# Reciprocal roots on VectorE, and a decoder's last FFN quantised in 16-bit steps

## The chip, the cores and the metric

The kernel runs on one core of a Trainium2 chip, as one launch. The metric is the device time of a launch in microseconds. The time before is 2435.77 us, the median of 3 runs (2435.06 to 2436.54). TensorE (PE) does matmuls and transposes, VectorE (DVE) and ScalarE (ACT) the work between them, GpSimd (POOL) a few steps, and SyncE's queue (SP) most weight loads.

## The reference

The program is a decoder of four layers on x of 8 sequences of 112 tokens and 256 features. Each layer is an attention, a cross attention on a context of 375 tokens, and an FFN, each added to x. Each begins with a layer norm without parameters:

```python
def _layernorm(x, axis=-1, eps=1e-05):
    m = jnp.mean(x, axis=axis, keepdims=True)
    v = jnp.var(x, axis=axis, keepdims=True)
    return (x - m) / jnp.sqrt(v + eps)
```

Some sublayers have norms of their own besides. The last FFN quantises its three weights and both its activations in blocks of 16 neighbours along the last axis:

```python
def fake_quant_nvfp4(x, global_scale):
    xb = x.reshape(sh[:-1] + (sh[-1] // BLOCK, BLOCK))
    amax = jnp.max(jnp.abs(xb), axis=-1, keepdims=True)
    sc = jnp.clip(amax / FP4_MAX * global_scale, 0.0, FP8_MAX)
    sc8 = sc.astype(jnp.float8_e4m3fn).astype(jnp.float32)
    dq = sc8 / global_scale
    safe_dq = jnp.where(dq == 0.0, 1.0, dq)
    a = jnp.clip(jnp.abs(xb) / safe_dq, 0.0, FP4_MAX)
    q = jnp.sign(xb) * _FP4_VALS[jnp.digitize(a, _FP4_MIDS)]
    return (q * dq).reshape(sh)
```

With gate and up of shape 1024 x 256 and down of 256 x 1024, it computes `x + linear(silu(gate(x)) * up(x), down)`, where each linear quantises both its inputs.

## The kernel before, in words

x stays in SBUF with the 112 tokens on the partitions and (sequence, feature) along the free axis. The twelve sublayers run one after the other.

**Order.** Tile's scheduler lays out each engine's instructions ahead of time. It goes by the program's order as priority, by its own estimates of when inputs are ready, and by when memory comes free. Inside a `manual_schedule` block the named engines keep the program's order; instructions from outside such a block can be put between. So statistics of the next norm (L431, L432) stand among the instructions of an attention that is still running.

**Norms.** `stats` (L424) takes mean and variance of each sequence by two DVE instructions, then calls `rsqrt` (L410) once for all the sequences that it was given. `normalise` (L442) subtracts and scales, one DVE instruction a sequence (L445). `rsqrt` adds eps (L414), takes the square root on ScalarE (L415), the reciprocal on DVE (L416), and a Newton step in four DVE instructions (L418 to L421). It runs 35 times: 32 times on 4 columns, twice on 8, once on 24. ScalarE's functions come from tables of which one set is active at a time; where the next function is in another set, an ACT_TABLE_LOAD is put ahead of it. Square root, Exp, Silu, Gelu and Sigmoid take turns, so 75 loads stand in the trace, 29 of them on L415.

**Quotients.** `quantise` (L1968) works on up to 2048 columns at once. Maxima of the blocks of 16 by one reduction (L1985); nine instructions on one column per block that round the scale to 8 bits and take its reciprocal (L1987 to L2001); the product of values and reciprocals, a block's factor broadcast over its 16 columns (L2004); a clamp (L2005); rounding to 4-bit values by adding and subtracting a number taken from the exponent (L2007 to L2010); the product with the scale, which writes bf16 (L2011). All of it is DVE's, and fp32 but for the last output.

**Last FFN** (`l3_ffn`, L2060). All eight sequences are normalised at once. Then x is quantised by halves of four sequences (1024 columns), transposed on PE and copied by ScalarE. Then come the four pairs of sequences: for each sequence and each half of the 1024 hidden columns, gate and up (four bf16 matmuls), Silu on ScalarE (L2103), and the product on DVE (L2104); `quantise` on the pair's 2048 columns; sixteen transposes (L2113), two copies (L2117), the down matmuls, and the sum into x (L2121). No order is written out by hand here. The output leaves by one DMA at the end.

**Weights of that FFN** are loaded by GpSimd's queue, quantised (`rounded`, L2023) and transposed (`turned`, L2040) while the third layer's last stages run. Their order along the free axis is set on the host (L250).

The cross attention ahead of the last FFN (`cross`, L1089) is one `manual_schedule` block; each sequence's result is added to x one sequence late, at L484.

Of the kernel before, what the change touches and what calls it, by code (L numbers as in the profile page):

```python
# [21 lines left out]
I32 = mybir.dt.int32  # L22
BF16 = mybir.dt.bfloat16
AF = mybir.ActivationFunctionType
ALU = mybir.AluOpType
# [4 lines left out]
P = 128  # L30
# [83 lines left out]
def _weights(inp):  # L114
# [134 lines left out]
    ]  # L249
    raw = [_fm(f("gate_w")), _fm(f("up_w")), _fm(f("down_w"))]  # L250
    v3 = [
# [101 lines left out]
class _Kernel:  # L353
# [56 lines left out]
    def rsqrt(self, var, rows, n):  # L410

        nc, small = self.nc, self.small
        va, sd, rs, t = (self.t(small, [P, 24], tag)[:rows, :n] for tag in ("va", "sd", "rs", "nt"))
        nc.vector.tensor_scalar(va, var, EPS, None, ALU.add)  # L414
        nc.scalar.activation(sd, va, AF.Sqrt)  # L415
        nc.vector.reciprocal(rs, sd)  # L416

        nc.vector.tensor_tensor(t, rs, rs, ALU.mult)  # L418
        nc.vector.tensor_tensor(t, t, va, ALU.mult)
        nc.vector.tensor_scalar(t, t, -0.5, 1.5, ALU.mult, ALU.add)  # L420
        nc.vector.tensor_tensor(rs, rs, t, ALU.mult)  # L421
        return rs
# [1544 lines left out]

    def quantise(self, pool, src, dst, rows, n, gs, amax=None):  # L1968


        nc = self.nc
        nb = n // 16

        def blocks(a):
            return a.rearrange("p (k e) -> p k e", e=16)

        def bc(a):
            return a[:, :, None].to_broadcast([rows, nb, 16])

        def sm(tag):  # L1980
            return self.t(pool, [P, nb], f"q{tag}{nb}")[:rows]

        if amax is None:
            amax = sm("m")
            nc.vector.tensor_reduce(amax, blocks(src), AX.X, ALU.max, apply_absolute_value=True)  # L1985
        sc, st, z = sm("s"), sm("t"), sm("z")
        nc.vector.tensor_scalar(sc, amax, 1.0 / 6.0, gs, ALU.mult, ALU.mult)  # L1987
        nc.vector.tensor_scalar(sc, sc, 448.0, None, ALU.min)


        big = 1.5 * 2.0**23
        nc.vector.tensor_scalar(
            st.bitcast(I32), sc.bitcast(I32), 0x7F800000, None, ALU.bitwise_and
        )
        nc.vector.tensor_scalar(st, st, 0.125 * big, 2.0**-9 * big, ALU.mult, ALU.max)
        nc.vector.tensor_tensor(sc, sc, st, ALU.add)
        nc.vector.tensor_tensor(sc, sc, st, ALU.subtract)
        nc.vector.scalar_tensor_tensor(z, sc, 0.0, sc, ALU.is_equal, ALU.add)
        nc.vector.reciprocal(z, z)

        nc.vector.tensor_scalar(z, z, gs, 1.0 + 2.0**-23, ALU.mult, ALU.mult)  # L2001
        a = self.t(pool, [P, n], f"qa{n}")[:rows]
        m = self.t(pool, [P, n], f"qm{n}")[:rows]
        nc.vector.tensor_tensor(blocks(a), blocks(src), bc(z), ALU.mult)  # L2004
        nc.vector.tensor_scalar(a, a, 6.0, -6.0, ALU.min, ALU.max)  # L2005

        nc.vector.tensor_scalar(m.bitcast(I32), a.bitcast(I32), 0x7F800000, None, ALU.bitwise_and)  # L2007
        nc.vector.tensor_scalar(m, m, 1.0, 0.5 * big, ALU.max, ALU.mult)
        nc.vector.tensor_tensor(a, a, m, ALU.add)
        nc.vector.tensor_tensor(a, a, m, ALU.subtract)  # L2010
        nc.vector.tensor_tensor(blocks(dst), blocks(a), bc(sc), ALU.mult)  # L2011

    def l3_weights(self, pool, ps):
# [9 lines left out]
        def rounded(i, nk, no):  # L2023
            amax = self.t(pool, [P, P], "amax")
            nc.vector.tensor_reduce(
                amax, raws[i].rearrange("p (k e) -> p k e", e=16), AX.X, ALU.max, apply_absolute_value=True
            )
            top, gs = (self.t(pool, [P, 1], n) for n in ("top", "gs"))
            nc.vector.tensor_reduce(top, amax, AX.X, ALU.max)
            nc.gpsimd.partition_all_reduce(gs, top, P, bass_isa.ReduceOp.max)  # L2030
            nc.vector.reciprocal(gs, gs)
            nc.vector.tensor_scalar(gs, gs, 448.0 * 6.0, None, ALU.mult)
            nc.vector.reciprocal(self.igs[:, i : i + 1], gs)
            wqs[i] = self.t(pool, [P, no, nk * P], "wq", BF16)
            flat = wqs[i].rearrange("p o k -> p (o k)")
            for h in range(2):
                cols = slice(h * 1024, (h + 1) * 1024)
                self.quantise(pool, raws[i][:, cols], flat[:, cols], P, 1024, gs, amax[:, h * 64 : (h + 1) * 64])

# [20 lines left out]
    def l3_ffn(self):  # L2060
# [3 lines left out]
        with ExitStack() as ctx:  # L2064
# [10 lines left out]
            for i, j in enumerate((0, 0, 1)):  # L2075
                nc.vector.tensor_tensor(sc[:, i : i + 1], self.igs[:, i : i + 1], inv[:, j : j + 1], ALU.mult)
            self.normalise(self.x, self.xn)
            xq = self.t(acts, [P, NB, D], "xq", BF16)
            xqT = self.t(acts, [P, 2, T], "xqT", BF16)
            for half in range(2):  # L2080
                bs = slice(half * HB, (half + 1) * HB)
                flat = [a[:S, bs, :].rearrange("p b d -> p (b d)") for a in (self.xn, xq)]
                self.quantise(pool, *flat, S, HB * D, s_in[:S])
                tp = self.t(ps, [P, 2, HT], "tr16", BF16)
                for kc in range(2):
                    for j in range(HB):
                        nc.tensor.transpose(
                            tp[:, kc, j * S : (j + 1) * S],
                            xq[:S, half * HB + j, kc * P : (kc + 1) * P],
                            self.ident16[:S, :S],  # L2090
                        )
                nc.scalar.copy(xqT[:, :, half * HT : (half + 1) * HT], tp)
            for b0 in range(0, NB, 2):
                hid = self.t(work, [P, 2, 1024], "hid")[:S]
                for j in range(2):
                    xb = self.tokens(b0 + j, xqT)
                    for i in range(2):
                        gu = self.t(ps, [P, 2, 512], "gu")
                        cols = slice(i * 512, (i + 1) * 512)
                        for n, m in enumerate((g, u)):  # L2100
# [3 lines left out]
                        nc.vector.scalar_tensor_tensor(  # L2104
                            hid[:, j, cols], gu[:S, 1, :], sc[:S, 1:2], sg, ALU.mult, ALU.mult
                        )
                hq = self.t(work, [P, 2, 1024], "hq", BF16)[:S]
                flat = [a.rearrange("p b d -> p (b d)") for a in (hid, hq)]
                self.quantise(pool, *flat, S, 2048, s_down[:S])
                for j in range(2):  # L2110
                    tp = self.t(ps, [P, 8, S], "tr16", BF16)
                    for c in range(8):
                        nc.tensor.transpose(  # L2113
                            tp[:, c, :], hq[:, j, c * P : (c + 1) * P], self.ident16[:S, :S]
                        )
                    hT = self.t(work, [P, 8, S], "hqT", BF16)
                    nc.scalar.copy(hT, tp)  # L2117
                    y = self.t(ps, [P, 512], "y")[:S, :D]
                    self.mm(y, [(hT[:, c, :], d[:, c, :]) for c in range(8)])
                    x = self.x[:S, b0 + j, :]  # L2120
                    nc.vector.scalar_tensor_tensor(x, y, sc[:S, 2:3], x, ALU.mult, ALU.add)  # L2121

# [35 lines left out]
```

## Time and profile before

| What | Value |
| --- | --- |
| Median of 3 runs | 2435.77 us (2435.06 to 2436.54) |
| Profiled execution | 2432.16 us |
| Its span | 2430.4 us |
| Granted clock of TensorE, mean | 0.954 |
| Busy share: PE, DVE, ACT, POOL | 88%, 59%, 34%, 9% |
| Square roots (L415): table loads, busy | 29, 37.2 us |
| Last sequence of the cross attention added to x | 2306.37 to 2306.79 us |
| Last sum into x | 2424.03 to 2424.51 us |
| DVE busy from 2308 to 2342 us | 32.65 of 34 us |

Times in a view are counted from the start of the span. A group's row gives line, engine, operation, output and inputs by name, shapes, count, then busy us and mean ns of one, then idle us of that engine just before. A row of the timeline gives start, us, engine and the instruction, and in brackets the idle time before it and who ended it. The chain of waits goes back from the last instruction to what released each one. A row of a stretch gives busy us and number of instructions of PE, PEld, DVE, ACT and POOL, the granted clock, and DMA.

### The profile page before, as it was taken

What the parts mean: (1) busy time and instruction counts of PE and PEld (TensorE: products, weight loads), DVE (VectorE), ACT (ScalarE), POOL (GpSimd) and SP (SyncE); (2) the same over time, 40 slices, a digit from 0 to 9 for tenths busy, and PEclk for the clock granted to TensorE, in tenths of its full rate; (3) what the DMA queues carried; (4) which work ended last, traced back from release to release, by engine and by line L of the source; (5) the groups of instructions that cost most, each with busy time, mean ns of one, the idle gap of its engine ahead of it and who ended that gap; (6) DMA issues with size and microseconds to landing.
All of it is one profiled execution on the core that took longest, in us unless ns stands there. A gap on an engine that the chain in (4) does not pass through costs nothing.

```text
span 2430.4 us, 43101 instructions
## 1 busy us (share of the span) xinstructions
PE 2138.1 (88%) x17032; PEld 1268.6 (52%) x17032; DVE 1434.3 (59%) x3810; ACT 826.8 (34%) x2220; POOL 215.8 (9%) x415
## 2 busy tenths in 40 slices
PE   6999999889899899899988859899999999899842
PEld 3444444455556566546555536466555556556622
DVE  4555556565446567553877547767740223667698
ACT  2333334453312356430111213467321111346521
POOL 0111111000011100000222331100000000100000
PEclk9999999999999999999999979999999999899966
DMA  4000000000100000100001011000111100000000
GB/s 185 2 2 2 2 20 35 29 18 18 52 1 15 18 1 2 36 26 18 35 18 35 18 28 52 17 2 19 53 35 62 41 1 1 1 1 2 2 1 15
DMA packets 10729, 55.93 MB, mean 23 GB/s; under 512 B 1833, under 2 KB 3625, under 8 KB 5792
## 3 DMA queue, kind: packets, MB, share of 16 engines
q1 hardware_dynamic: 8304, 44.57, 5.1%
q0 software_dynamic: 2080, 7.07, 0.9%
q8 instruction: 135, 2.21, 0.4%
q10 hardware_dynamic: 144, 1.54, 0.2%
q14 instruction: 66, 0.54, 0.1%
HBM read 52.23 MB, written 0.92 MB: 22 GB/s over the span
## 4 chain that ended last, share of the span: by engine, by line
PE 66%; DVE 22%; issue 5%; ACT 4%; DMA 2%; POOL 1%; DVEq 0%; ACTq 0%; POOLq 0%
PE mm L407 31%; PE tr L1178 6%; PE gu L407 6%; PE g L640 6%; PE sc L407 4%; PE av L1194 3%; PE tr L407 1%; DVE rot L1487 1%; PE av L777 1%; ACT sg L651 1%; PE av L407 1%; ACT th L662 1%; PE s L407 1%; DVE hT L666 1%; DMA cx<-in_ctx 1%
## 5 line engine op out<-in xcount | busy, mean ns | idle before, releaser
L640 PE MATMUL g<-w,hT 128*32 128x256 f32 x3552 | 237.4, 384 | 26.0 <-DVE hT L666 24.6
L1178 PEld LDWEIGHTS tr<-cst,xe 112*125 112x125 f32 x1152 | 151.5, 188 | 96.7 <-issue 37.0
L1165 DVE TENSOR_REDUCE xnm<-sc 112x1 f32<-112x375 f32 x384 | 184.3, 540 | 29.5 <-PE sc L407 28.9
L1178 PE MATMUL tr<-cst,xe 112*125 112x112 f32 x1152 | 193.1, 289 | 8.6 <-DVE xeT L1186 3.5
L407 PE MATMUL mm<-xnT,w 128*128 128x448 f32 x432 | 183.0, 559 | 19.7 <-DVE qT L1490 4.5
L407 PE MATMUL mm<-hT,w 128*128 128x448 f32 x512 | 193.0, 539 | 0.0
L640 PEld LDWEIGHTS g<-w,hT 128*32 128x32 f32 x3552 | 95.7, 109 | 167.5 <-DVE hT L666 124.6
L407 PEld LDWEIGHTS mm<-hT,w 128*128 128x128 f32 x512 | 97.1, 190 | 94.4 <-issue 94.4
L1186 DVE COPY xeT<-tr 125x336 f32<-125x336 f32 x192 | 97.3, 507 | 70.4 <-PE tr L1178 63.0
L618 PE MATMUL g<-xw,cst 128*32 128x256 f32 x1792 | 138.7, 379 | 0.0
L1184 ACT COPY xeT<-tr 125x336 f32<-125x336 f32 x192 | 85.0, 443 | 155.8 <-PE tr L1178 155.8
L407 PE MATMUL mm<-w,hT 128*112 128x256 f32 x576 | 132.6, 389 | 0.0
L407 PEld LDWEIGHTS mm<-xnT,w 128*128 128x128 f32 x432 | 77.8, 193 | 102.8 <-issue 52.6
L1169 ACT ACTIVATE xe<-sc,xnm 112x375 f32<-112x375 f32 x256 | 126.2, 581 | 9.5 <-DVE xnm L1165 9.2
L407 PE MATMUL mm<-w,oT 128*112 128x256 f32 x416 | 105.8, 405 | 24.0 <-DVE oT L1667 15.2
L407 PE MATMUL gu<-xnT,w 128*128 128x448 f32 x320 | 124.4, 544 | 1.7 <-DVE hT L1332 1.2
L407 PEld LDWEIGHTS mm<-w,hT 128*112 128x112 f32 x576 | 103.7, 182 | 27.5 <-issue 4.8
L651 ACT ACTIVATE sg<-g 128x192 f32<-128x192 f32 x224 | 73.9, 330 | 105.4 <-PE g L640 94.1
L662 ACT ACTIVATE th<-cell 128x64 f32<-128x64 f32 x224 | 57.5, 257 | 147.2 <-DVE cell L660 147.1
L407 PEld LDWEIGHTS mm<-w,oT 128*112 128x112 f32 x416 | 73.9, 186 | 54.1 <-DVE oT L1667 16.3
L664 DVE TENSOR_TENSOR h<-sg,th 128x64 f32<-128x64 f32 x224 | 50.4, 225 | 84.8 <-ACT th L662 84.8
L2046 DVE COPY wq<-tr 128x256 bf16<-128x256 bf16 (+1 forms) x12 | 4.6, 420 | 157.5 <-PE tr L2045 157.5
(398 smaller groups left out, 3673.3 us busy)
## 6 DMA issues: line engine op xcount, KB each, us to landing
w<-in_w SPq DMA_DIRECT2D x33, 1024.0 KB, 4.9
raw<-in_wq POOLq DMA_DIRECT2D x3, 1024.0 KB, 5.3
w<-in_w SPq DMA_DIRECT2D x3, 896.0 KB, 6.4
wi<-in_wint POOLq DMA_DIRECT2D x3, 768.0 KB, 5.6
w<-in_w SPq DMA_DIRECT2D x2, 768.0 KB, 4.2
ctxT<-in_ctxT ACTq DMA_DIRECT2D x1, 1500.0 KB, 8.3
cx<-in_ctx POOLq DMA_DIRECT2D x1, 1500.0 KB, 22.5
w<-in_w SPq DMA_DIRECT2D x2, 512.0 KB, 3.5
```

The lines of the kernel that those rows point to most:

```text
L407: self.nc.tensor.matmul(out, lhsT, rhs, start=i == 0, stop=i == len(pairs) - 1)
L618: nc.tensor.matmul(g[32 * j : 32 * j + 32, :], pick[:, t % 16, :], xw[:, l, t // 16, 256 * j : 256 * j + 256], start=True, stop=t == 0, sk ...
L640: nc.tensor.matmul(g[32 * j : 32 * j + 32, :], hT[l][:, c, :], whh[l][:, c, 256 * j : 256 * j + 256], start=False, stop=c == 1, skip_group ...
L651: nc.scalar.activation(sg[:, :192], g[:, :192], AF.Sigmoid)
L662: nc.scalar.activation(th, cell[l], AF.Tanh)
L664: nc.vector.tensor_tensor(h, og, th, ALU.mult)
L1165: nc.vector.tensor_reduce(nm, sc, AX.X, ALU.max, negate=True)
L1169: nc.scalar.activation(e, sc, AF.Exp, bias=nm)
L1178: nc.tensor.transpose(tp[:CH, i * S : (i + 1) * S], e[:, i * CH : (i + 1) * CH], self.ident[:S, :S])
L1184: nc.scalar.copy(eT, src)
L1186: nc.vector.tensor_copy(eT, src)
L1194: nc.tensor.matmul(avs[b][32 * j : 32 * j + 32, c * S : (c + 1) * S], values[b % 2][:CH, i, 4 * c + j, :], eTs[b, c, j][:, i, :], start=i ...
```

## The change

**`rsqrt`** no longer uses ScalarE. It takes a first guess from the bits of the variance (a shift by one and a subtraction), improves it by a parabola and a Newton step, ten DVE instructions in all with the one that adds eps.

**`quantise`** works on another order of columns: within each row of 256 or 1024 the 16 members of a block lie apart, at equal places of 16 runs. For that the host permutes rows and columns of the weights, the norm of x writes with a stride, and the weights' maxima are reduced with a stride. Maxima of activations come from magnitudes that ScalarE makes (`Abs`), halved four times by DVE. After the first product only the high 16 bits are kept, with the lowest set to 1; the clamp, the rounding and the last product are on bf16, and the scale is bf16 as well. The last product is made 1024 columns at a time. `quantise` is a generator that yields between its steps.

**`l3_ffn`** normalises by halves, and writes the order of its pairs out by hand: between the steps of one pair's quotients stand the four pieces of the next pair's hidden values, the sums into x of the pair before, and, after each half of the last product, that sequence's transposes and matmuls.

```diff
-        va, sd, rs, t = (self.t(small, [P, 24], tag)[:rows, :n] for tag in ("va", "sd", "rs", "nt"))
-        nc.vector.tensor_scalar(va, var, EPS, None, ALU.add)
-        nc.scalar.activation(sd, va, AF.Sqrt)
-        nc.vector.reciprocal(rs, sd)
-
-        nc.vector.tensor_tensor(t, rs, rs, ALU.mult)
-        nc.vector.tensor_tensor(t, t, va, ALU.mult)
-        nc.vector.tensor_scalar(t, t, -0.5, 1.5, ALU.mult, ALU.add)
-        nc.vector.tensor_tensor(rs, rs, t, ALU.mult)
+        va, r0, w, p, rs = (self.t(small, [P, 24], tag)[:rows, :n] for tag in ("va", "r0", "rw", "rp", "rs"))
+        vec = nc.vector
+        vec.tensor_scalar(va, var, EPS, None, ALU.add)
+        vec.tensor_scalar(r0.bitcast(I32), va.bitcast(I32), 1, None, ALU.logical_shift_right)
+        vec.tensor_scalar(r0.bitcast(I32), r0.bitcast(I32), -1.0, float(0x5F300000), ALU.mult, ALU.add)
+        root = 0.446405130**0.5
+        vec.scalar_tensor_tensor(w, r0, root, va, ALU.mult, ALU.mult)
+        vec.tensor_tensor(w, w, r0, ALU.mult)
+        vec.scalar_tensor_tensor(p, w, -1.38883461 / root, w, ALU.add, ALU.mult)
+        vec.scalar_tensor_tensor(p, p, 1.94247540, r0, ALU.add, ALU.mult)
+        vec.scalar_tensor_tensor(w, p, -0.5, va, ALU.mult, ALU.mult)
+        vec.tensor_tensor(w, w, p, ALU.mult)
+        vec.scalar_tensor_tensor(rs, w, 1.5, p, ALU.add, ALU.mult)
...
+    def block_max(self, pool, src, rows, n, row):
+
+        nb, k = n // 16, row // 16
+        e, a = 16, src.rearrange("p (r e k) -> p r e k", e=16, k=k)
+        while e > 1:
+            e //= 2
+            out = self.t(pool, [P, nb * e], f"qm{nb * e}")[:rows]
+            o = out.rearrange("p (r e k) -> p r e k", e=e, k=k)
+            self.nc.vector.tensor_tensor(o, a[:, :, :e, :], a[:, :, e : 2 * e, :], ALU.max)
+            a = o
+        return out
...
         if amax is None:
-            amax = sm("m")
-            nc.vector.tensor_reduce(amax, blocks(src), AX.X, ALU.max, apply_absolute_value=True)
-        sc, st, z = sm("s"), sm("t"), sm("z")
+            amax = self.block_max(pool, mag, rows, n, row)
+            yield
+        sc, st, z, s16 = sm("s"), sm("t"), sm("z"), sm("h", BF16)
...
-        nc.vector.tensor_tensor(sc, sc, st, ALU.subtract)
-        nc.vector.scalar_tensor_tensor(z, sc, 0.0, sc, ALU.is_equal, ALU.add)
+        nc.vector.tensor_tensor(s16, sc, st, ALU.subtract)
+        nc.vector.scalar_tensor_tensor(z, s16, 0.0, s16, ALU.is_equal, ALU.add)
         nc.vector.reciprocal(z, z)
-
         nc.vector.tensor_scalar(z, z, gs, 1.0 + 2.0**-23, ALU.mult, ALU.mult)
+        yield
         a = self.t(pool, [P, n], f"qa{n}")[:rows]
-        m = self.t(pool, [P, n], f"qm{n}")[:rows]
-        nc.vector.tensor_tensor(blocks(a), blocks(src), bc(z), ALU.mult)
-        nc.vector.tensor_scalar(a, a, 6.0, -6.0, ALU.min, ALU.max)
-
-        nc.vector.tensor_scalar(m.bitcast(I32), a.bitcast(I32), 0x7F800000, None, ALU.bitwise_and)
-        nc.vector.tensor_scalar(m, m, 1.0, 0.5 * big, ALU.max, ALU.mult)
-        nc.vector.tensor_tensor(a, a, m, ALU.add)
-        nc.vector.tensor_tensor(a, a, m, ALU.subtract)
-        nc.vector.tensor_tensor(blocks(dst), blocks(a), bc(sc), ALU.mult)
+        b, m = (self.t(pool, [P, n], f"q{i}{n}", BF16)[:rows] for i in "bp")
+        nc.vector.tensor_tensor(wide(a), wide(src), bc(z), ALU.mult)
+        yield
+        high = a.bitcast(I16).rearrange("p (n two) -> p n two", two=2)[:, :, 1]
+        nc.vector.tensor_scalar(b.bitcast(I16), high, 1, None, ALU.bitwise_or)
+        yield
+        nc.vector.tensor_scalar(b, b, 6.0, -6.0, ALU.min, ALU.max)
+
+        nc.vector.tensor_scalar(m.bitcast(I16), b.bitcast(I16), 0x7F80, None, ALU.bitwise_and)
+        nc.vector.tensor_scalar(m, m, 1.0, 96.0, ALU.max, ALU.mult)
+        yield
+        nc.vector.tensor_tensor(b, b, m, ALU.add)
+        nc.vector.tensor_tensor(b, b, m, ALU.subtract)
+        yield
+        for at in range(0, n, 1024):
+            part = slice(at, at + 1024)
+            half = s16[:, at // 16 : at // 16 + 64].rearrange("p (r k) -> p r k", k=k)
+            nc.vector.tensor_tensor(
+                wide(dst[:, part]), wide(b[:, part]),
+                half[:, :, None, :].to_broadcast([rows, 64 // k, 16, k]), ALU.mult,
+            )
+            yield
...
             nc.vector.tensor_reduce(
-                amax, raws[i].rearrange("p (k e) -> p k e", e=16), AX.X, ALU.max, apply_absolute_value=True
+                amax.rearrange("p (r k) -> p r k", k=nk * 8),
+                raws[i].rearrange("p (r e k) -> p r k e", e=16, k=nk * 8),
+                AX.X, ALU.max, apply_absolute_value=True,
             )
...
-            self.normalise(self.x, self.xn)
...
+                mv, rs = self.stats(self.x[:, bs, :], S, HB)
+                for j in range(HB):
+                    nc.vector.tensor_scalar(
+                        self.xn[:S, b0 + j, :].rearrange("p (e k) -> p k e", e=16),
+                        self.x[:S, b0 + j, :].rearrange("p (k e) -> p k e", e=16),
+                        mv[:S, j, 0:1], rs[:, j : j + 1], ALU.subtract, ALU.mult,
+                    )
                 flat = [a[:S, bs, :].rearrange("p b d -> p (b d)") for a in (self.xn, xq)]
-                self.quantise(pool, *flat, S, HB * D, s_in[:S])
+                mag = self.t(pool, [P, 2, 1024], "mag")[:S, 0, :]
+                nc.scalar.activation(mag, flat[0], AF.Abs)
+                for _ in self.quantise(pool, *flat, S, HB * D, D, s_in[:S], mag=mag):
+                    pass
...
+                        nc.scalar.activation(mags[b0][:, j, cols], hids[b0][:, j, cols], AF.Abs)
+                        yield
...
+            with tc.manual_schedule(engines={ET.PE, ET.DVE, ET.Activation}):
+                for _ in hidden(0):
+                    pass
+                for b0 in range(0, NB, 2):
+                    later = hidden(b0 + 2) if b0 + 2 < NB else iter(())
...
+                    for step, _ in enumerate(self.quantise(pool, *flat, S, 2048, 1024, s_down[:S], mag=mag)):
+                        if step == 1 and b0 > 0:
+                            add(b0 - 2)
+                            add(b0 - 1)
+                        if step >= 2:
+                            next(later, None)
+                        if step >= 6:
+                            result(b0 + step - 6, hq[:, step - 6, :])
+                add(NB - 2)
+                add(NB - 1)
```

## The prediction

> **What bounds the kernel now.** I read the page first, for the shares and the slices.
>
> ```profile
> PE 2138.1 (88%) x17032; PEld 1268.6 (52%) x17032; DVE 1434.3 (59%) x3810; ACT 826.8 (34%) x2220; POOL 215.8 (9%) x415
> ...
> PE   6999999889899899899988859899999999899842
> DVE  4555556565446567553877547767740223667698
> ```
>
> TensorE bounds nearly all of it; only in the last two slices (60.8 us each) does PE fall to 4 and 2 while DVE stays at 9 and 8. So I took the busy time by stretches (us, then PE, PEld, DVE, ACT, POOL): 2240 to 2260 is the last cross attention, the next two are the last FFN.
>
> ```profile
> 2240.00:2260.00 20.00, 19.64 (x212) 13.86 (x212) 14.88 (x35) 12.62 (x28) 0.61 (x1) 1.00 0.00 1
> ...
> 2342.00:2364.00 22.00, 9.44 (x41) 5.33 (x41) 21.76 (x21) 5.39 (x8) 0.00 (x0) 0.71 0.00 0
> 2364.00:2386.00 22.00, 8.79 (x44) 6.15 (x43) 21.59 (x28) 3.09 (x4) 0.00 (x0) 0.66 0.00 1
> ```
>
> Two regimes: the attention is PE's (98%), the FFN is DVE's (98%). A DVE microsecond is worth a microsecond after 2307, and in the attention only what it makes PE wait. Then the groups of instructions in the FFN, and the line of the roots.
>
> ```profile
> L2004 DVE TENSOR_TENSOR qa<-hid,qz 112x2048 f32<-112x2048 f32 x4 | 9.2, 2292 | 0.1
> L2011 DVE TENSOR_TENSOR hq<-qa,qs 112x2048 bf16<-112x2048 f32 x4 | 9.2, 2291 | 0.1
> L2009 DVE TENSOR_TENSOR qa<-qa,qm 112x2048 f32<-112x2048 f32 x4 | 9.2, 2288 | 0.1
> ...
> L1985 DVE TENSOR_REDUCE qm<-hid 112x128 f32<-112x2048 f32 x4 | 9.1, 2280 | 0.0
> ...
> L2005 DVE TENSOR_SCALAR qa<-qa 112x2048 f32<-112x2048 f32 x4 | 4.9, 1224 | 0.1
> ```
>
> Two-input and reducing operations take nearly twice what the one-input L2005 takes for the same 2048 columns, and DVE's idle time before each (last column, us) is nil. For the roots I took line 415's instructions (duration in ns: least, median, most), the chain of waits around one root (start, us, what), and the last root in order of time:
>
> ```profile
> L415 ACT ACT_TABLE_LOAD  x29: 1283/1283/1283, 1.2 to 2298.6; - x29
> ```
>
> ```profile
> 1301.37 1.28 ACT L415
> 1302.65 0.01 issue
> 1302.66 0.21 ACT sd L415
> ```
>
> ```profile
> 2307.50 0.17 DVE L414 TENSOR_SCALAR va<-mv 112x8 f32<-112x8 f32 x1
> 2307.71 0.21 ACT L415 ACTIVATE sd<-va 112x8 f32<-112x8 f32 x1 [7.80 <-DVE va L414]
> 2307.95 0.20 DVE L416 RECIPROCAL rs<-sd 112x8 f32<-112x8 f32 x1 [0.28 <-ACT sd L415]
> 2308.19 0.17 DVE L418 TENSOR_TENSOR nt<-rs 112x8 f32<-112x8 f32 x1
> ```
>
> At 1301 the root waits for a load of ScalarE's table; at 2307 it doesn't, and what is left is a chain of small dependent steps, one every 0.2 us.
>
> **The change, part by part.** The profiled execution took 2432.16 us (span 2430.4 and 1.8 around it); the median is 3.6 above. Sums are made against 2432.2 and then shifted by 3.6. Each DVE duration below carries the 0.04 us between dependent instructions that the timeline shows.
>
> *Quotients of a pair of sequences (2048 columns, 4 times).* Before: L1985 2.32; nine small steps 3.39 (2402.00 to 2405.39); two one-tensor-broadcast products 2.33 each; add and subtract 2.33 each; three one-input steps 1.26 each: 18.8. After: the maximum by four halvings in fp32 (1024, 512, 256, 128 columns: rows of those widths take 1.22, 0.69, 0.42, 0.29) 2.78; small steps 3.39; first product, still fp32, 2.33; a new OR that takes the high halves. The rest is 16-bit, and no row of this trace has a 16-bit source and target in SBUF. Here the Trainium skill, page "VectorE: DVE Perf Modes", section "The perf-mode tier table (the rule you actually need)", gives for 2048 columns: one-input 693 ns in bf16 against 1227 in fp32, two-input 1224 against 2293. Its fp32 figures are the rows' 1224 and 2288, so I take its bf16 ones. The OR reads every second 16-bit element; between 0.73 and 2.33 I take the nearest row, the one-input 1.26. Then three one-input steps at 0.73, add and subtract at 1.26, two last products of 1024 columns at 0.73: 2.78+3.39+2.33+1.26+2.19+2.52+1.46 = 15.9. By the rule -2.8 a pair, -11.3 in all; by the rows' fp32 rates instead +0.46 (maximum) +1.26 (OR) +0.04 = +1.8 a pair, +7.0.
>
> *Quotients of a half (1024 columns, twice).* Likewise 11.2 becomes 10.0: -2.3 in all; by the rows' rates +2.5.
>
> *Norm of the FFN.* It is split by halves. Half 0's needs only four sequences, done by 2240, so its statistics, roots and four xn (some 4.5 us of DVE) move into the attention. DVE is idle 5.1 of 20 us there, in gaps of 0.4 to 0.8 us; an instruction that overruns a gap delays PE. Cover holds in part: +1.0 (0 to +4.5). After the last x (2306.8) remain one root and four xn with stride 64 bytes. Contiguous they take 0.34 (8 in 2.67); no row has such a write, and the skill's "Vector Engine (DVE) Microarchitecture Reference", section 5.2, has 2.50 ns per column for scattered writes, so 0.8 at most; I take 0.6, between. 2.05+2.4 against 1.49+2.67: +0.3.
>
> *ScalarE's Abs and the added order.* Sixteen Abs of 512 columns at some 0.63 (between 576 ns for 448 columns in SBUF, L498, and 687 for 512 with a scale from memory, L2103) and two of 1024 at 1.06 are 12 us on an engine that is busy 5.4 and 3.1 of 22 us in the stretches above: hidden, but they add waits. Abs of a piece waits for DVE's hid; behind it in ScalarE's queue stands the next Silu, for which the next hid waits: 0.61+0.69 and three hand-overs, 1.4, against the OR's 1.26 that DVE has in between: +0.2 in three pairs, +0.6. There is one buffer for magnitudes: pair 0's first Abs waits until half 1's maxima have read it, and pair 0's other three pieces, some 2.2 each, run behind that; DVE has 8 us of half 1 left then, so nothing, and up to 2 if it hasn't. Relu (L703) has no load of its own before it in the rows, so I take none for Abs. The four pieces of the next pair now stand at fixed places in DVE's queue, ahead of the next steps of the quotients: where a piece is late, the quotients wait. PE needs some 14 us of a pair's 19 for them and the results, so I take nothing.
>
> *End.* Before, 16 transposes ran in a row after the last quotient, and 5.4 us passed to the last x (2419.1 to 2424.5). Now sequence 7's transposes stand in PE's queue behind sequence 6's matmuls, which wait for ScalarE's copy: 1.03 (transposes) +0.95 (copy) +1.4 (matmuls), then again 1.03+0.95+1.99+0.48, less the 0.7 by which the first starts earlier: 7.1. +1.7. In earlier pairs the next 6 us of quotients cover this.
>
> *Weights.* Their quotients (1737 to 2000) lie beside PE work. Their maxima now read with stride: 2.28 to at most 5.1 each (same 2.50 ns). The first, at 1727, stands ahead of an xnT that PE takes next: +1.0 (0 to +2.8). DMAs are the same in number and size; no step passes SP's or POOL's queue.
>
> *35 roots.* One ACT and six DVE instructions become ten DVE ones of 0.16 to 0.17 (the 112x8 rows of this kernel), 2.05 us where 1.46 is the bare chain now: +0.59 each. Summed along the chain of waits, the six lines hold 15.3 us, 2.55 a line: four more lines +10.2. Off the chain come sd 1.83 and the loads that only the root needs: L415 3.85 (three), Exp's reload at L752 1.28 and L498 1.79: -8.75. Some 47 of 75 loads go. The rule that would make them dearer is in "ScalarE: Activation LUTs", "What ACT_TABLE_LOAD costs": 1283 ns plus a drain of some 1380. The rows agree with 1283, but the next ACTIVATE starts 0.01 us later (1302.66 above): the drain would save another 7, and I leave it out. Off the chain, Exp's reloads at 944, 1659 and 2106 have 1.1, 0.9 and 2.0 us of idle PE beside them: -4.0. Net -2.5, from -9 to +6, as every new DVE order in the attentions moves PE waits.
>
> Sum: -11.3 -2.3 +0.3 +1.0 +0.6 +1.7 +1.0 -2.5 = -11.5: 2420.7, and with 3.6 the median 2424.
>
> **The rivals.** *Half 0 is quantised early (2417).* From 2298 to 2307 DVE is idle for 6.9 us while the attention drains. Half 0's quotients could go there, another -7. For it: its inputs are ready. Against: `inv` (L2073), which waits for no data, ran only at 2298.1, just when the attention's values were last read, so tiles of the FFN wait for the attention's memory, and the later ones lie over buffers read until 2306.
>
> *The roots eat the gain (2433).* If the reloads' idle PE is filled by the four extra dependent instructions, the roots cost +6 and not -2.5. Against: at 1301, 1490 and 2120 the load itself is in the chain.
>
> *The 16-bit steps run no faster than fp32 (slower, 2447).* Place: after 2307. If views with a stride, a broadcast or an in-place target miss the fast modes, the quotients give +7.0+2.5 in place of -13.6: 23.1 us worse, sum +11.6. It decides from the point where half of that 23.1 is lost. For it: no such row in the trace. Against: the last operands are contiguous over 64 columns, and the fp32 rows follow the table to 0.3%.
>
> **Chances.** Likeliest case 0.50 (2419 to 2429), early half 0.28 (2411 to 2419), roots 0.13 (2429 to 2438), no modes 0.09 (2438 to 2450). Range 2408 to 2434: it takes in the early half, with roots at their better end, and half of the roots' case. A measurement tells about 0.2% (4.9 us) from no change: faster (below 2430.9) 0.82, within 0.10, slower 0.08.
>
> **What would show it.** The pairs' one-input 16-bit rows at 0.7, add and subtract at 1.22, last products at 0.7, OR at 1.2; from one hq to the next 19 us where 21.2 stand now; loads about 28; ten rows of 0.16 per root. I am wrong if the OR or the products take over 2 us, if half 0's quotients stand before 2306, or if PE's idle time in the attentions moves by more than 6 us.

## The result, and the profile after

| What | Before | Changed |
| --- | --- | --- |
| Median, first comparison (6 runs each) | 2435.41 us | 2417.14 us |
| Ratio, with 95% interval | | 0.9927 (0.9910 to 0.9944): 17.8 us faster |
| Profiled execution, span | 2432.16, 2430.4 us | 2413.31, 2411.5 us |
| Table loads on ScalarE | 75 | 29 |
| Last x of the cross attention added | 2306.79 us | 2297.07 us |
| From there to the last sum | 117.7 us | 108.5 us |

The forecast was 2424, within 2408 to 2434: the time lies inside, and the change gave 18 us where the sum said 11.5. A second comparison of the same two kernels, later and with 22 runs of the changed one, gave a ratio of 0.9964 (0.9953 to 0.9976), 8.8 us. What moves the time of unaltered code that far is shown below; the sum lies between the two. The median of the first comparison, 2417.14, lies outside the prediction's likeliest case (2419 to 2429); that of the second, 2421.13, lies in it.

First come the busy shares and the slices of the changed kernel's page.

```profile
PE 2138.1 (89%) x17032; PEld 1268.5 (53%) x17032; DVE 1430.9 (59%) x3994; ACT 773.9 (32%) x2157; POOL 217.1 (9%) x415
...
PE   6999999989898899899898859899999999899944
DVE  4655566565545567553888557767750133667787
```

DVE is as busy as before, with 184 instructions more; ScalarE has lost 53 us. The stretches of the last FFN (us, then PE, PEld, DVE, ACT, POOL, clock):

```profile
2342.00:2364.00 22.00, 12.80 (x59) 8.88 (x58) 20.61 (x33) 7.66 (x11) 0.00 (x0) 0.66 0.00 1
2364.00:2386.00 22.00, 11.73 (x61) 8.43 (x59) 20.44 (x37) 7.66 (x11) 0.00 (x0) 0.66 0.00 0
```

DVE still sets the pace, but is no longer full: 20.6 and 20.4 of 22 us where 21.8 and 21.6 stood. The groups of that stage (busy, mean ns):

```profile
L2030 DVE TENSOR_TENSOR qa<-hid,qz 112x2048 f32<-112x2048 f32 x4 | 9.1, 2284 | 0.0
...
L2046 DVE TENSOR_TENSOR hq<-qb,qh 112x1024 bf16<-112x1024 bf16 x8 | 5.1, 684 | 0.0
...
L2033 DVE TENSOR_SCALAR qb<-qa 112x2048 int16<-112x2048 int16 x4 | 4.9, 1220 | 0.0
L2040 DVE TENSOR_TENSOR qb<-qb,qp 112x2048 bf16<-112x2048 bf16 x4 | 4.9, 1217 | 0.0
...
L2178 DVE SCALAR_TENSOR_TENSOR x<-y,sc,x 112x256 f32<-112x256 f32 x8 | 3.9, 482 | 8.6 <-PE y L410 8.6
...
L2035 DVE TENSOR_SCALAR qb<-qb 112x2048 bf16<-112x2048 bf16 x4 | 2.7, 685 | 0.0
```

These are the forecast prices: 0.69 us for one input in 16 bits (L2035), 1.22 for add and subtract (L2040) and for the OR with its stride (L2033), 0.68 for a last product in spite of its broadcast scale (L2046). The row to look at is that of the sums into x, L2178: 8.6 us of DVE waiting for TensorE, 6.7 of them at the end and the rest within the pairs. The last root begins like this, in order of time:

```profile
2298.39 0.16 DVE L418 TENSOR_SCALAR va<-mv 112x4 f32<-112x4 f32 x1
2298.51 0.42 DVE L1985 TENSOR_TENSOR qm<-qm 112x256 f32<-112x256 f32 x1
2298.85 0.16 DVE L421 TENSOR_SCALAR r<-va 112x4 int32<-112x4 int32 x1
```

Its steps alternate with half 0's maxima and small steps, so neither chain waits for its own results. Half 0's quotients did not run ahead of the last x, which was added by 2297.07:

```profile
2296.69 1.06 ACT L2134 ACTIVATE mag<-xn 112x1024 f32<-112x1024 f32 x1 [6.42 <-PE mm L410]
```

Their inputs were ready by 2238.3, but their `Abs`, shown here, was released by the last matmul of the attention.

The stretch from the last x to the last sum, by its own marks (us):

| Part | Before | Changed | Difference |
| --- | --- | --- | --- |
| last x to the last quotient of half 1 | 28.4 | 20.7 | -7.7 |
| to the first product of pair 0 | 10.9 | 12.3 | +1.5 |
| to the last quotient of pair 3 | 73.0 | 67.8 | -5.2 |
| to the last sum | 5.4 | 7.7 | +2.3 |
| all | 117.7 | 108.5 | -9.2 |

The other 9.7 us of the profiled pair lie ahead of the last x.

### The profile page after: what moved, and what is told of

Same layout as the page of the kernel before. It is cut to its first block, busy times and chain, and to the rows that moved or that the text cites. A ratio compares the mean times of both kernels' runs of the same rounds, so it can differ in the third digit from the quotient of the medians.

```text
span 2411.5 us, 43235 instructions
## 1 busy us (share of the span) xinstructions
PE 2138.1 (89%) x17032; PEld 1268.5 (53%) x17032; DVE 1430.9 (59%) x3994; ACT 773.9 (32%) x2157; POOL 217.1 (9%) x415
## 4 chain that ended last, share of the span: by engine, by line
PE 67%; DVE 21%; issue 5%; ACT 4%; DMA 2%; POOL 1%; DVEq 0%; ACTq 0%; POOLq 0%
PE mm L410 31%; PE gu L410 6%; PE g L649 6%; PE tr L1187 6%; PE sc L410 4%; PE av L1203 3%; PE tr L410 2%; DVE rot L1496 1%; ACT sg L660 1%; PE av L786 1%; PE av L410 1%; ACT th L671 1%; DVE hT L675 1%; PE g L627 1%; PE s L410 1%
## 5 line engine op out<-in xcount | busy, mean ns | idle before, releaser
L410 PE MATMUL mm<-xnT,w 128*128 128x448 f32 x432 | 182.3, 559 | 18.8 <-DVE qT L1499 5.3
```

The costliest lines, as they stand in the source:

```text
L410: self.nc.tensor.matmul(out, lhsT, rhs, start=i == 0, stop=i == len(pairs) - 1)
```

## Experiments

Times against before are worked out from ratio and interval. The runs e1 to e4, f1 to f4 and g1 to g4 ran on three chips, each beside the kernel before on the same chip (medians 2435.1, 2431.6 and 2431.0 us). The column "stretch" is the trace's time from the last x to the last sum: the unaltered changed kernel gave 108.52 and 108.50 in two executions, so tenths can be read there. The whole time doesn't allow that: f2, f3, f4 and g1 do not stand clear of the changed kernel in it (-17.8 and -8.8), and what they gain is shown by the stretch alone.

| Run | What | Against before, us | Stretch, us |
| --- | --- | --- | --- |
| e1 | root alone | -4.4 (-7.1 to -1.9) | 119.5 |
| e2 | all but the root | -5.1 (-7.1 to -3.2) | 108.7 |
| e3 | unread square roots | -1.2 (-3.2 to +1.0) | 108.9 |
| e4 | root without its Newton step | -24.4 (-27.5 to -21.2) | 107.9 |
| f1 | steps in fp32 | +5.6 (+2.4 to +8.8) | 124.3 |
| f2 | Abs later | -14.3 (-19.2 to -9.5) | 105.8 |
| f3 | transposes first | -12.6 (-17.0 to -8.0) | 104.1 |
| f4 | sums later | -10.7 (-14.6 to -6.8) | 107.5 |
| g1 | half 0 early | -12.4 (-17.0 to -7.8) | 97.6 |
| g2 | Abs and transposes | -17.3 (-22.6 to -11.7) | 101.2 |
| g3 | g1 and g2 | -22.6 (-27.7 to -17.7) | 91.9 |
| g4 | the changed kernel again | -8.8 (-11.4 to -5.8) | 108.5 |

### The two parts apart (e1, e2)

e1 is the kernel before with the ten-step `rsqrt`; e2 is the changed kernel with the old one.

> The kernel before with the new root alone; the last FFN as before. Theory A (from the two traces: matmuls of the changed kernel start 8.6 us earlier at 2060 and 9.2 at 2200, of which the roots are the only cause up to 1700): 8 to 9 us faster than before, some 29 table loads left of 75. Theory B (the prediction's sum: four more dependent DVE steps per root eat most of it): 2.5 us faster, between 0 and 4.

> The changed kernel with the old root (Sqrt, reciprocal, Newton step). Theory A: the last FFN with its weights gives 9 to 10 us, so 9 to 10 us faster than before. Theory B: 15 to 16 us faster, since the roots would give only 2.5 of the 18. If the two parts feed each other (half 0's root in the cross attention brings a table load there), less than 9.

The root alone gave 4.4 us: theory B's 2.5 lies in the interval, theory A's 8 to 9 doesn't. The rest gave 5.1, less than either theory; that it might be less than 9 was the third case. Part of both shortfalls is the clock, as the section on g4 shows. In e2's stretch all of the FFN's gain is there (108.7), so the rest is lost earlier. One place is the feed-forward ahead. ScalarE and TensorE of e2:

```profile
1767.19 0.21 ACT L418 ACTIVATE sd<-va 112x4 f32<-112x4 f32 x1 [3.57 <-DVE va L417]
1767.42 1.28 ACT L1753 ACT_TABLE_LOAD   x1
```

```profile
1769.40 6.09 PE L410 MATMUL mm<-xnT,w 128*128 128x448 f32 x11 [3.02 <-ACT hT L1753]
```

The square root stands in ScalarE's queue for 3.6 us until DVE, busy with the weights' maxima (now 3.61 us each), has written `va`; the next evacuation stands behind it, and TensorE waits 3.0 us for that. The other place is half 0's root in the cross attention: it takes two table loads there, and the sequence takes 22.19 us where the others take 19.49, +2.70 (20.32 with the new root, +0.83). In e2 TensorE's granted clock is halved for 3.41 us of that sequence, which it isn't in the changed kernel:

```profile
2257.60:2261.01 3.41, 3.41 (x33) 2.07 (x29) 2.25 (x6) 1.95 (x5) 0.16 (x1) 0.50 0.02 5
```

TensorE is busy all through it, and at the full clock the same work would take half as long, 1.7 us (an estimate); so most of the difference of 1.9 can be the clock. So the FFN's change is dearer with a root that uses ScalarE, by 3.0 us at the first place and by 1.9 at the second, clock and waits together.

### The price of loads and of steps (e3, e4)

```diff
         vec.tensor_scalar(va, var, EPS, None, ALU.add)
+        sd = self.t(small, [P, 24], "sd")[:rows, :n]
+        nc.scalar.activation(sd, va, AF.Sqrt)
```

> The changed kernel with one more ScalarE instruction per root: a square root of the variance that nothing reads, so the table loads come back (about 75) but no root waits for them. Theory A: the loads were worth it because other ScalarE work (Exp, Silu) waited for their reload: 4 to 8 us slower than the changed kernel, near 2422. Rival: the loads cost only where the root itself waited (three places in the chain, 3.85 us), and the reloads were hidden: within 1 us of the changed kernel.

With 77 loads the changed kernel is 7.6 us slower than by the second comparison and 16.6 than by the first: more than theory A's 4 to 8 at one end, and the rival's 1 us is out. No DVE instruction reads these roots, so none of it is a root that waits for its own load: it is other work that waits behind ScalarE's queue, and a clock that is halved for longer. In the traces the last x comes 21.4 us later than in the changed kernel's first execution. Worked out as in the section on g4, the clock is 11.1 of that and the waits are 10.2.

e4 leaves out the step's three instructions:

```diff
-        vec.scalar_tensor_tensor(p, p, 1.94247540, r0, ALU.add, ALU.mult)
-        vec.scalar_tensor_tensor(w, p, -0.5, va, ALU.mult, ALU.mult)
-        vec.tensor_tensor(w, w, p, ALU.mult)
-        vec.scalar_tensor_tensor(rs, w, 1.5, p, ALU.add, ALU.mult)
+        vec.scalar_tensor_tensor(rs, p, 1.94247540, r0, ALU.add, ALU.mult)
```

> The changed kernel without the Newton step of the root (three of the ten DVE instructions left out, so the roots are only approximate). It prices a dependent step. By the chain of the changed kernel (2.2 us a line over 35 roots): 6 to 7 us faster than the changed kernel, near 2410. Rival, steps mostly lie beside PE work: 0 to 3 us faster.

With 4 runs it is 6.6 us faster than the changed kernel by the first comparison and 15.6 by the second, so the whole time cannot size it. The stretch is 0.6 us shorter, three steps of 0.2. With the clock taken off, as in the section on g4, the last x comes 5.3 us earlier than in the mean of six executions of the changed kernel's code. Together that is 5.9, next to theory A's 6 to 7 and above the rival's 3; it rests on one execution, and those six spread over 5.4.

### What moves the whole time (g4)

> The changed kernel once more, unaltered, on the chip of the three others: how far an unaltered kernel's time moves, and what they are set against. 14 to 20 us faster than before by the first comparison (17.8, interval 13.6 to 21.9); the stretch from the last x to the last sum within 0.3 us of 108.5.

The stretch held, the whole time didn't: 8.8 us for 17.8. The two executions of the same code differ only ahead of the last x, which is added at 2297.07 in one and 2305.35 in the other, and they part in jumps. Two stretches, of the first and of the second (the clock is the last but two):

```profile
440.00:460.00 20.00, 18.50 (x56) 8.00 (x56) 5.97 (x10) 7.88 (x24) 0.00 (x0) 0.66 0.00 0
...
1000.00:1020.00 20.00, 17.05 (x76) 11.37 (x75) 7.26 (x22) 4.07 (x5) 0.62 (x1) 0.74 0.00 1
```

```profile
440.00:460.00 20.00, 17.71 (x93) 8.63 (x91) 8.12 (x16) 10.19 (x35) 0.00 (x0) 1.00 0.00 0
1000.00:1020.00 20.00, 17.09 (x57) 11.46 (x58) 6.82 (x22) 1.13 (x3) 0.61 (x1) 0.57 0.00 0
```

TensorE's granted clock differs: 0.66 against 1.00 at 440, 0.74 against 0.57 at 1000. The clock records of the traces show the pattern. From moment to moment the clock is either 1.0 or 0.5, and in all fourteen traces every change of it falls on a grid of 3.41 us, to 0.01 us. The grid lies differently against the first instruction from one execution to the next. Here are stretches cut along it, the first two of the changed kernel, then two of g4:

```profile
441.43:444.84 3.41, 1.94 (x7) 0.89 (x8) 1.28 (x2) 0.63 (x1) 0.00 (x0) 1.00 0.00 0
444.84:458.49 13.65, 13.65 (x36) 5.99 (x34) 3.89 (x6) 5.10 (x13) 0.00 (x0) 0.50 0.00 0
```

```profile
439.43:442.84 3.41, 3.02 (x9) 1.19 (x7) 0.42 (x1) 0.98 (x2) 0.00 (x0) 1.00 0.00 0
442.84:446.25 3.41, 2.30 (x8) 0.89 (x8) 1.50 (x3) 0.29 (x1) 0.00 (x0) 1.00 0.00 0
```

Both executions have the same two gaps on TensorE there, 0.72 and 0.77 us. In the changed kernel's both lie in one step of the grid, which leaves 1.94 us busy of 3.41, and the clock is halved for the next 13.65 us. In g4's an edge of the grid cuts the first gap, the steps are busy for 3.02 and 2.30 us, and the clock stays. The Trainium skill, "TensorE: Matmul & The Clock Gate", section "What's actually happening", calls the window in which activity is counted free-running. That makes the same gap cheap or dear by where it falls, as these stretches show.

What this costs can be worked out from TensorE's busy time while its clock is halved. These are the sums of all such stretches up to the last x, of the kernel before, the changed kernel and g4:

```profile
sum 136.33, PE 106.98 PEld 68.46 DVE 57.84 ACT 27.97 POOL 10.60; mean PE 5.09 PEld 3.26 DVE 2.75 ACT 1.33 POOL 0.50
sum 131.92, PE 107.03 PEld 67.50 DVE 58.22 ACT 22.92 POOL 16.93; mean PE 5.10 PEld 3.21 DVE 2.77 ACT 1.09 POOL 0.81
sum 145.62, PE 119.34 PEld 75.65 DVE 63.42 ACT 21.46 POOL 18.57; mean PE 5.42 PEld 3.44 DVE 2.88 ACT 0.98 POOL 0.84
```

If a matmul takes twice as long at half the clock, half of this time is what the clock added. The traces bear that out: all fourteen run the same 16824 matmuls up to the last x, busy for 2092.5 to 2107.8 us, and less that half they lie between 2037.8 and 2041.5. The code up to the last x, and each engine's order of instructions, is the same in six of these kernels:

| | before | changed | f4 | g4 | f2 | g2 | f3 |
| --- | --- | --- | --- | --- | --- | --- | --- |
| PE busy at half clock, us | 107.0 | 107.0 | 106.6 | 119.3 | 119.2 | 123.3 | 139.5 |
| last x at, us | 2306.8 | 2297.1 | 2297.3 | 2305.3 | 2304.2 | 2305.8 | 2310.0 |
| last x less half of the first row | 2253.3 | 2243.6 | 2244.0 | 2245.7 | 2244.6 | 2244.2 | 2240.3 |

In the six, the last x moves over 13 us and the half moves over 16; what is left lies within 5.4 us, and within 2.1 but for f3, where the half takes off too much, as slower matmuls also fill waits. So the clock moves the whole time. At an even clock the last x of the changed kernel comes some 9.6 us earlier than before (2243.7 in the mean of the six), that of e1 8.5 (2244.8), and that of e2 not at all (2253.4).

The whole times agree. In this second comparison the mean granted clock was 0.955 in the 27 executions of before and 0.951 in the 22 of the changed kernel. Within either kernel, executions whose mean clock is 0.001 lower take 2.3 to 2.4 us more, so 0.004 are some 9 us (an estimate): what this comparison gave less than the first. Beside e1 and e2 before had 0.952, and they 0.951. Whether the changed code makes such a clock more likely, or the grid fell so, is not shown.

### The fast modes (f1)

```diff
-        high = a.bitcast(I16).rearrange("p (n two) -> p n two", two=2)[:, :, 1]
-        nc.vector.tensor_scalar(b.bitcast(I16), high, 1, None, ALU.bitwise_or)
...
-        nc.vector.tensor_tensor(b, b, m, ALU.add)
-        nc.vector.tensor_tensor(b, b, m, ALU.subtract)
+        nc.vector.tensor_tensor(a, a, m, ALU.add)
+        nc.vector.tensor_tensor(a, a, m, ALU.subtract)
```

> The changed kernel with the quotients' steps in fp32 again (no OR; clamp, mask, add, subtract on fp32 in the new order of columns; the halving maxima, ScalarE's Abs and the written order stay). If the 16-bit rows (0.69 one-input, 1.22 two-input for 2048 columns) carry the FFN's gain: each pair 0.54x3 + 1.06x2 - 1.22 (the OR goes) + last products twice 1.22 for 0.65 each, about +3.6 a pair and +1.8 a half, some 16 us more than the changed kernel (near 2433), and from one first product to the next 23 us for 19.4. Rival, the written order and the moved norm carry it: within 4 us of the changed kernel.

The stretch grew by 15.7 us, and from one first product to the next it takes 22.4 us for 19.4; the 16-bit rows carry the gain. With the OR that f1 does not need (1.26 by four and 0.7 by two, 6.4) it would be some 22 us (an estimate), near the 23.1 that the third rival put at stake. That rival is out.

### Three waits in the last FFN (f2, f3, f4, g2)

Ahead of pair 0's maxima DVE of the changed kernel waits for one piece after the other, and ScalarE shows why:

```profile
2320.49 0.75 DVE L2161 SCALAR_TENSOR_TENSOR hid<-gu,sc,sg 112x512 f32<-112x512 f32 x1 [2.01 <-ACT sg L2160]
2322.51 0.75 DVE L2161 SCALAR_TENSOR_TENSOR hid<-gu,sc,sg 112x512 f32<-112x512 f32 x1 [1.27 <-ACT sg L2160]
2323.96 1.23 DVE L1985 TENSOR_TENSOR qm<-mag 112x1024 f32<-112x1024 f32 x1 [0.70 <-ACT mag L2164]
```

```profile
2321.27 0.63 ACT L2164 ACTIVATE mag<-hid 112x512 f32<-112x512 f32 x1 [0.82 <-DVE hid L2161]
2321.81 0.67 ACT L2160 ACTIVATE sg<-gu,sc 112x512 f32<-112x512 f32 x1
```

The hidden value (0.75), its Abs (0.63) and the next Silu (0.67) that stands behind it form a loop of 2.0 us a piece. f2 issues each Abs behind the next Silu:

```diff
                         nc.scalar.activation(sg, gu[:S, 0, :], AF.Silu, scale=sc[:S, 0:1])
+                        if late is not None:
+                            nc.scalar.activation(*late, AF.Abs)
...
-                        nc.scalar.activation(mags[b0][:, j, cols], hids[b0][:, j, cols], AF.Abs)
+                        late = (mags[b0][:, j, cols], hids[b0][:, j, cols])
+                        if j and i:
+                            nc.scalar.activation(*late, AF.Abs)
```

> The changed kernel with each Abs issued one piece later, behind the next Silu, in ScalarE's queue. Theory: pair 0's pieces come every 2.0 us because hid, Abs, Silu and hid follow each other in one chain, and DVE waits 4.0 us there; with Abs behind the next Silu they come every 1.4 us or so: about 2 us faster than the changed kernel, DVE's idle time ahead of pair 0's maxima down from 4.0 to some 2. Rival: TensorE at its low clock (1.02 us a piece) or the free PSUM buffers set the 2.0, nothing changes.

The pieces start 1.3, 1.4 and 2.2 us apart, DVE's idle time from the last x to pair 0's first product falls from 5.1 to 3.3 us, and the stretch by 2.7.

The end of the changed kernel on TensorE, and that of f3, which puts both sequences' transposes first:

```profile
2397.39 0.93 PE L2170 MATMUL tr<-ident,hq 112*128 112x112 bf16 x8 [9.47 <-DVE hq L2046]
2399.36 1.96 PE L410 MATMUL y<-wq,hqT 128*112 128x256 bf16 x8 [1.05 <-ACT hqT L2172]
2401.11 0.95 PE L2170 MATMUL tr<-ident,hq 112*128 112x112 bf16 x8
2403.12 1.96 PE L410 MATMUL y<-wq,hqT 128*112 128x256 bf16 x8 [1.05 <-ACT hqT L2172]
```

```profile
2408.14 1.68 PE L2170 MATMUL tr<-ident,hq 112*128 112x112 bf16 x16 [11.26 <-DVE hq L2046]
2410.12 3.47 PE L410 MATMUL y<-wq,hqT 128*112 128x256 bf16 x16 [0.30 <-ACT hqT L2172]
```

```diff
                         if step >= 6:
-                            result(b0 + step - 6, hq[:, step - 6, :])
+                            across(b0 + step - 6, hq[:, step - 6, :])
+                        if step == 7:
+                            result(b0)
+                            result(b0 + 1)
```

> The changed kernel with both sequences' transposes ahead of both sequences' matmuls in TensorE's queue. Theory: at the end the second sequence's transposes stand behind the first one's matmuls, which wait for ScalarE's copy; the 7.65 us from the last quotient to the last x become some 5.4 to 6 as before the change: 2 us faster than the changed kernel. Rival, the low clock is what makes the end long: within 0.5 us.

One wait for ScalarE's copy is gone: 5.4 us at the end for 7.7. The stretch fell by 4.4, twice what was expected, since a pair now takes 18.7 us for 19.4: the sums no longer wait for the second sequence either. f4 moves the sums into x behind the first product instead:

```diff
-                        if step == 1 and b0 > 0:
+                        if step == 2 and b0 > 0:
```

> The changed kernel with the sums into x one step later, behind the next pair's first product. DVE waits 0.64 us for the second sequence's matmuls in three pairs; behind the 2.3 us product it should not: 1.9 us faster than the changed kernel, from one first product to the next 18.8 us for 19.4. Rival: the wait only moves to another place in the pair, 0.

1.0 us, half of what was expected; DVE's idle time within the four pairs falls from 4.1 to 3.0, of the 1.9 us of those waits 0.8 came back elsewhere.

> The changed kernel with both edits, Abs behind the next Silu and both sequences' transposes ahead of both their matmuls. Alone they took 2.7 and 4.4 us from the stretch between the last x of the attention and the last sum (108.5 us). If they act at different places: 101.4 us there, 7 us faster than the changed kernel. If they share a wait: 103 to 104.

101.2: the two act at different places.

### Half 0 in memory of its own (g1, g3)

```diff
-            xq = self.t(acts, [P, NB, D], "xq", BF16)
+            early = _Carved(self.w)
+            xqs = [self.t(early, [P, HB * D], "xq0", BF16), self.t(acts, [P, HB * D], "xq1", BF16)]
...
-                for _ in self.quantise(pool, *flat, S, HB * D, D, s_in[:S], mag=mag):
+                for _ in self.quantise(pool if half else early, *flat, S, HB * D, D, s_in[:S], mag=mag):
```

`_Carved` cuts tiles from buffers of the weight ring.

> The changed kernel with half 0's quotients, their scratch and their result in memory of the weight ring that no longer holds weights, in place of memory that the cross attention still uses. Theory: half 0's quotients waited for nothing but that memory (its Abs at 2296.69 was released by the attention's last matmul), so its first product moves from 2303 to before 2290, and from the last x of the attention to the last sum 108.5 us become 97 to 101, for 1 to 3 us more in the attention: 6 to 9 us faster than the changed kernel. Rival: the quotients fill DVE's gaps in the attention and make TensorE wait as much as they save: within 2 us.

The first product of half 0 moved from 2302.7 to 2256.1 and the stretch fell by 10.9 us to 97.6: it was the memory that had held it. But the price is higher than the 1 to 3 us expected: the attention's sequence in which the quotients run takes 24.85 us for 20.32, and the last two together 0.9 more. Up to 1.7 us of it can be the clock, which is halved within that sequence here (in g3 too) and not in the changed kernel:

```profile
2258.71:2262.12 3.41, 3.41 (x16) 2.22 (x9) 3.13 (x8) 1.62 (x4) 0.00 (x0) 0.50 0.00 0
```

Net 5.5 us by the trace; the whole times give 3.6 against g4, with overlapping intervals.

> The three edits together: half 0's quotients in memory of their own, Abs behind the next Silu, both sequences' transposes first. If they add up: 92 to 95 us from the last x of the attention to the last sum where the changed kernel has 108.5, near 2403. With half 0 early pair 0's pieces no longer wait on Abs at the bound, then the Abs edit adds nothing: 95 to 97.

91.9 us, 16.6 less than the changed kernel, and the whole time 2405.52 against g4's 2421.13 on the same chip: the fastest version with a complete root, 22.6 us (17.7 to 27.7) faster than before. Part of that is the clock, 0.957 in the mean of its executions and 0.951 in g4's. Against g1 it is 5.7 less in the stretch, of which f3's edit alone took 4.4; if it does so here too, 1.3 of the 2.7 us of the Abs edit remain with half 0 early.

## Why the prediction was right, and where it was off

**The bound, and the price list.** Right. DVE sets the FFN's time and TensorE the rest. The last pair's quotients take 17.1 us from the first maximum to the last product; 1.5 of it are the sums with their wait, so 15.6, where 15.9 was forecast and 18.8 stood. The prices for bf16 from the Trainium skill, "VectorE: DVE Perf Modes", section "The perf-mode tier table (the rule you actually need)", held to 2% (0.69 and 1.22 us).

**What the pairs gained.** Off by the waits. 3.2 us in each of four pairs are 12.8, more than the 11.3 of the sum (18.8 less 15.9 in four pairs is 11.5 by its own terms), but the written order gave part of it back at two places. The step "pair 0's other three pieces run behind that; DVE has 8 us of half 1 left then, so nothing" failed: DVE idles 4.0 us there, because quotients that are shorter and brought forward no longer cover the pieces, and Abs had made the pieces slower. And the sums into x wait 0.64 us in each of three pairs, which was not forecast.

**Halves and norm.** Forecast -2.0 together, against -7.7 by the marks. That part is not like for like: before, three hidden values and the start of a fourth lay in it, in the changed kernel one and the start of a second, 1.3 us. The rest, some 4 us, comes by the timeline from two independent chains in turn on DVE, 0.12 us a step for 0.20, which the sum left out; no run shows it alone.

**The end.** 7.7 us for 7.1, right in kind and mechanism; f3 showed it.

**Moved work.** Half 0's norm in the attention cost 0.83 us (forecast 1.0). The weights' strided maxima took 3.61 us each, between the bounds 2.28 and 5.1. They cost TensorE 3.0 us at one place where a square root stood in ScalarE's queue (e2), and with the new root the lead of the matmuls over those of before grew instead, by 1.0 from 1700 to 1800.

**Early half 0.** This rival gave the very number that the first comparison measured, 2417, but it did not happen. The argument against it was right, as g1 showed: the tiles waited for the attention's memory. The number was met by other means, which is luck. Half 0's first product did stand ahead of 2306, the prediction's sign of being wrong, but only because the last x itself came at 2297; it ran at 2302.7, behind it.

**The roots.** The sign was right, and the rival that they eat the gain (+6) is out: the sum said -2.5, from -9 to +6, and alone they gave -4.4 (-7.1 to -1.9). The mis-sized term is the steps. The sum put four more lines of 2.55 us on the chain, +10.2. The DVE lines of the root held 15.3 us there before and hold 22.5 now, 2.25 a line: +7.2. With that the sum would have said -5.5. At an even clock e1's last x comes 8.5 us earlier, so that sum is still too small. What the sum took off for square roots and loads, 12.75 us, lies within the 7.6 to 16.6 that giving them back cost in e3, and above the 10.2 that e3's waits cost at an even clock. What the sum did not have is that a square root holds ScalarE's queue until DVE has come to it, as e2 shows; it counted loads alone, and the 3.0 us of TensorE's waiting there are its one measured size.

**The size.** Of the 7.3 us by which the profiled execution beat the sum (18.85 for 11.5), the stretch of the FFN goes the other way (-9.2 for -11.0). The rest lies ahead of the last x, -9.7 for -0.5, and it is not the clock: both executions of that pair were busy at half clock for 107.0 us, and six executions of the changed code give -9.6 at an even clock. So the roots and the moved work, -0.5 in the sum, are the terms that were sized too small. With the steps at 2.25 us and half 0 at 0.83 the sum would say -3.7 there. For the other 6 us the record has one cause, the square roots that hold ScalarE's queue; how much each place gave stays open. TensorE's idle time up to the last x fell from 211.8 to 204.5 us, 7.3; the prediction had named 6, in the attentions, as a sign of being wrong.

At an even clock the change is thus worth some 19 us, 9.6 and 9.2 (an estimate; of before there is one trace). The two comparisons gave 17.8 and 8.8 of it.

## What to carry to other kernels

Before pricing a step that moves off an engine, look at what stands behind it in that engine's queue: a small instruction that waits for another engine holds up everything after it, and that was worth more here than its own duration. When the bounding engine gets faster, list what its old work covered, since first pieces, hand-overs and the end become bare. A change of one per cent spread over a program is better read from a stretch that repeats to 0.02 us than from the whole time; where the matmuls are the same, first take off what TensorE's lower clock added in each trace.

## What the runs showed of the hardware

- The same code's last x moved by 13 us with TensorE's granted clock, with one core running. That clock was 1.0 or 0.5 and changed only on a grid of 3.41 us, which lay differently against the program from one execution to the next: after the same two gaps of 0.72 and 0.77 us it was halved for 13.65 us in one and stayed at 1.0 in another.
- A max reduction of 2048 columns whose reads jump takes 3.61 us, 1.76 ns a column, against 2.28 contiguous. In the Trainium skill, "Vector Engine (DVE) Microarchitecture Reference", section "Measured stream behaviour on trn2 (trn3 not measured)", this is near the row for one source that hops 4 KiB at every element (1.73), though the hops here are 64 or 256 bytes, and not the 2.50, for steps of 24 words, that the prediction took as its bound.
- A one-input 16-bit operation that reads every second element takes 1.22 us for 2048 columns, what fp32 takes, against 0.69 contiguous; a 16-bit product with a broadcast middle dimension takes 0.68 us for 1024 columns, where the fp32 one took 1.22.
